# A two-layer graph attention kernel: two small steps of layer 1 move from VectorE to GpSimd

## The chip, the cores and the metric

The kernel runs on one core of a Trainium2 chip. A core has five engines that run their own queues of instructions in order and meet through semaphores: TensorE (matrix products, PE in the profile; its weight loads are PEld), VectorE (DVE), ScalarE (ACT), GpSimd (POOL) and SyncE (SP). Transfers between the chip's memory and the on-chip buffer run on 16 DMA engines. Plain transfers are issued here from SyncE's and ScalarE's queues, gathers by index from GpSimd's. The metric is the device time of one execution in microseconds (us).

## The reference

The reference is one residual block of a graph network: 10,000 nodes with 768 features, 160,000 edges and a self loop per node (each layer adds one more), twice a graph attention layer, and a layer norm over the sum of input and output.

```python
def gat_conv(x, edge_index, W, a_src, a_dst, bias, heads, out_ch, concat):
    ei = _add_self_loops(edge_index, n)
    src, dst = (ei[0], ei[1])
    xl = (x @ W).reshape(n, heads, out_ch)
    alpha_src = jnp.einsum('nhc,hc->nh', xl, a_src)
    alpha_dst = jnp.einsum('nhc,hc->nh', xl, a_dst)
    e = jax.nn.leaky_relu(alpha_src[src] + alpha_dst[dst], 0.2)
    m = jax.ops.segment_max(e, dst, num_segments=n)
    e = jnp.exp(e - m[dst])
    s = jax.ops.segment_sum(e, dst, num_segments=n)
    alpha = e / (s[dst] + 1e-16)
    msg = xl[src] * alpha[:, :, None]
    out = jax.ops.segment_sum(msg, dst, num_segments=n)
...
h = gat_conv(x, edge_index, W1, a_src1, a_dst1, b1, HEADS, HID, True)     # 4 heads of 256
h = jax.nn.relu(layer_norm(h, g1, be1)) + (h0 @ Wr1 + br1)
h1 = h
h = gat_conv(h, edge_index, W2, a_src2, a_dst2, b2, 1, OUT_DIM, False)    # 1 head of 768
h = layer_norm(h, g2, be2) + (h1 @ Wr2 + br2)
...
x = _layernorm(x + h)
```

For every node the sources of its incoming edges are looked up, their projected rows are weighted by a softmax over those edges, and summed.

## The kernel before

The work has three stages, one after the other. All of it is in float32.

**Preparation** (to about 890 us). The nodes are sorted by their number of incoming edges and dealt into 79 tiles of 128 nodes, one node a partition; all nodes of a tile get the same number of places, `SLOTS[t]`, which is that of its largest node. Small tiles have 9 to 14 places, the middle ones 15 to 20, and the largest 21 to 41. `slots` is an integer array with a column for each place of each tile: which row the place is to fetch. Meanwhile `x @ W1` is computed tile by tile and written to `table1`, one row a node. Such a row has R1 = 1033 numbers: 1024 of the projected node, 4 logits as a destination, 4 logits as a source, and in the last column the node's rank in the sorted order, negated.

**Layer 1** (`ordered_layer1`, about 890 to 3,395 us). The tiles are taken in an order that goes from the small ones to the largest and back to small ones (`TURNS`). For a tile, each place's 128 rows are fetched by one gather (`gather`, L425, on GpSimd's queue) into one slot of a ring of 29 slots (`Ring`). The ring runs ahead of the work: when a slot's row has been used, `ring.fetch` issues the gather that refills it with the row 29 places later. A gather therefore waits for the last instruction that reads the slot's old row.

`logits` (L473) forms, over all places of a tile, the sum of source and destination logits (L479), the leaky ReLU (L189), the maximum (L483), the difference (L486) and, on ScalarE, the exponential (L487). It then handles two things for later, in each contiguous part of the ring that the tile's rows take (one part, or two where the ring wraps): the last column of the gathered rows is turned into integers and put into `slots` (L490), so that layer 2 fetches by rank from its own sorted table; and the last five columns of the slots, source logits and rank, are set to a large negative number (L491), so that a later place that fetches no row weighs nothing. `normalised` divides by the sum (L498 to L504).

Of a tile's rows, the first one to four (`on_pe`) are summed on TensorE with diagonal matrices of their weights (diagonals by ScalarE, L730; products, L736). The other rows are added on VectorE by `weigh`: one in four by four multiply-adds straight from the ring (L521), the other three by an addition (L517) after ScalarE has multiplied the row by its weights (L510). After a tile's sum come its layer norm and residual on VectorE (L579 to L595, L807), the transposes of the result (L708, L709), and the products with the layer-2 weights (L829). The residual's product with `Wr1` (L172) runs on TensorE as well.

The order on each engine's queue is that of the program text; no scheduler moves anything. The text sets the weights of the next tile early, while the present one still has three rows to weigh:

```python
if n - LEAD <= k < n - LEAD + 2:
    ready += itertools.islice(ahead, 1)     # first logits of t + 1, then its normalised weights
if k >= first:
    weigh(acc, ring.slot(FIRST[t] + k), e[:, k], DH1, shared=shared(t, k))
ring.fetch(FIRST[t] + k + 1 + ring.size)
```

The one tile with more places than the ring has slots (41) goes through `attend_parts`, which calls `logits` for a part of its places at a time.

**Layer 2** (`ordered_layer2`, to the end). It fetches rows of its own table by the rewritten `slots`, with a ring of 41 slots whose own-node rows come by plain transfers; there `ring.own` holds entries, and the two steps of L490 and L491 are left out. A second path for graphs that don't fit the sorted form (`general_path`) isn't taken with these inputs.

Of the kernel before, what the change touches and what calls it, by code (L numbers as in the profile page):

```python
# [32 lines left out]
OP = mybir.AluOpType  # L33
# [4 lines left out]
BIG = 1.0e30  # L38
# [42 lines left out]
def gnn_kernel(ctx, tc, x, x_cols, src, dst, src_col, dst_col, W1, a_src1, a_dst1, b1, g1, be1, Wr1, br1,  # L81
               W2, a_src2, a_dst2, b2, g2, be2, Wr2, br2, out, n_edges):
    nc = tc.nc
# [6 lines left out]
    R1, R2 = C1 + 2 * H1 + 1, C2 + 2 * H2  # L90
    NT = -(-N // P)
    NP = NT * P
# [40 lines left out]
    slots = consts.tile([P, TOTAL], I32, name="slots")  # L133
# [54 lines left out]
    def leaky(to, a):  # L188
        nc.vector.scalar_tensor_tensor(to, a, SLOPE, a, op0=OP.mult, op1=OP.max)  # L189
# [283 lines left out]
    def logits(small, ring, lo, hi, ad, heads, c, top=None):  # L473


        n = hi - lo
        e = small.tile([P, ring.size, heads], F32, name="e")[:, :n]
        for a, b, rows in ring.parts(lo, hi):
            nc.vector.tensor_tensor(e[:, a - lo:b - lo], rows[:, :, c + heads:c + 2 * heads],  # L479
                                    ad[:, None, :].to_broadcast([P, b - a, heads]), op=OP.add)  # L480
        leaky(e, e)
        new = small.tile([P, heads], F32, name="new")
        nc.vector.reduce_max(new, e.rearrange("p k h -> p h k"), axis=AX.X)  # L483
        if top is not None:
            nc.vector.tensor_max(new, new, top)
        nc.vector.tensor_tensor(e, e, new[:, None, :].to_broadcast([P, n, heads]), op=OP.subtract)  # L486
        nc.scalar.activation(e, e, AF.Exp)  # L487
        for a, b, rows in ring.parts(lo, hi):
            if not ring.own:
                nc.vector.tensor_scalar(slots[:, a:b], rows[:, :, R1 - 1], -1.0, float(NP), op0=OP.mult, op1=OP.min)  # L490
                nc.vector.memset(rows[:, :, c + heads:], -BIG)  # L491
        return e, new

    def normalised(small, e, heads, t):
# [29 lines left out]
    def attend_parts(small, ring, acc, h_, ad, heads, dh, t, summed, between):  # L524
# [6 lines left out]
        nc.vector.memset(acc[:, :c], 0.0)  # L531
        for lo, hi in zip(cuts, cuts[1:]):
            e, new = logits(small, ring, lo, hi, ad, heads, c, top)
            if lo == FIRST[t]:
                doubled(e, t)
# [150 lines left out]
    def ordered_layer1():  # L686
        nc.scalar.add_instruction(mybir.InstLoadActFuncSet(name=nc.get_next_instruction_name(), act_func_set_id=6, engine=nc.scalar.engine))
        with tc.tile_pool(name="b1", bufs=1) as pool, tc.tile_pool(name="small1", bufs=2) as small, \
# [52 lines left out]
            def weights_of(t):  # L741

                n, m = SLOTS[t], on_pe(t)
                e, _ = logits(small, ring, FIRST[t], FIRST[t] + n, ring.slot(FIRST[t])[:, C1:C1 + H1], H1, C1)
                yield e
                normalised(small, e, H1, t)
                acc = ps_acc.tile([P, 2 * BANK], F32, name="acc")
                diagonals = pool.tile([P, ON_PE1 * H1, P], F32, name="diagonals")
                for lo, hi in ((0, min(m, 2)), (min(m, 2), m)):
                    summed(acc, diagonals, e, FIRST[t], lo, hi, m)  # L750
                    yield acc
# [129 lines left out]
    def ordered_layer2():  # L881
# [6 lines left out]
        with tc.tile_pool(name="b2", bufs=1) as pool, tc.tile_pool(name="small2", bufs=2) as small, \  # L888
# [44 lines left out]
            def weights_of(t):  # L933
# [15 lines left out]
                def add_b2():  # L949
                    nc.tensor.matmul(to, ones, b2_b[0:1, ON_PE2:], start=False, stop=False, skip_group_check=True)  # L950

                e, top = logits(small, ring, at, at + cuts[1], ad, H2, C2)
                yield {0: (e, None)}
                if len(cuts) == 2:
# [387 lines left out]
```

## Time and profile before

| | |
|---|---|
| median of 3 runs | 5602.67 us (5597.33 to 5605.57) |
| profiled execution | 5607.1 us, span from first to last instruction 5605.3 us |
| TensorE, weight loads, VectorE | 4888.6 (87%), 2899.2 (52%), 4294.8 us (77%) busy |
| ScalarE, GpSimd | 2813.9 (50%), 3242.1 us (58%) busy |
| granted TensorE clock, mean | 0.93 |
| gathers into the ring (both layers) | 2675, 0.994 us each on GpSimd |
| L490 and L491 on VectorE | 124 each, 24.4 and 13.0 us |
| transfers | 1591 MB, 284 GB/s in the mean |

A group row of the profile gives line, engine, operation, the tiles written and read, their shapes and how often; after the bar the busy time and the mean of one in ns; after the second bar how long the engine had been idle just before such instructions, and what ended that idle time ("issue" is nothing that the profile shows). The shares are means over the three stages. In layer 1 VectorE's share is about 92% in most stretches of 100 us, and TensorE's 93 to 98% in many.

### The profile page before, as it was taken

How to read it: one execution, taken by the hardware profiler on the slowest of the kernel's cores; microseconds unless marked ns; L12 is line 12 of the kernel's file. 1: busy time of each engine (PE TensorE's matmuls, PEld its weight loads, DVE VectorE, ACT ScalarE, POOL GpSimd, SP SyncE). 2: the span in 40 equal slices, each digit the busy share in tenths (PEclk: the TensorE clock that was granted, in tenths of full speed). 3: DMA queues.
4: the chain of work that ended last, by engine and by line, in shares of the span. 5: the costliest groups of instructions: out<-in, count | busy, mean ns of one | idle time of the engine just before them, and what ended most of it. 6: DMA issues, size and time to landing. Idle time of an engine off the chain costs nothing. (4 is left out here: it accounts for less than half of the span.)

```text
span 5605.3 us, 59627 instructions
## 1 busy us (share of the span) xinstructions
PE 4888.6 (87%) x15188; PEld 2899.2 (52%) x15191; DVE 4294.8 (77%) x7761; ACT 2813.9 (50%) x8193; POOL 3242.1 (58%) x3159
## 2 busy tenths in 40 slices
PE   8999996999999875789999999899988888877765
PEld 3444443555555543455555555565655555555544
DVE  5783344999999887888999995888876866766676
ACT  3443344777788776777877773333322322222222
POOL 3447365556666556566666553666665666666664
PEclk9999998999999987899999999999998888888877
DMA  4333626999999987899999986999888888888885
GB/s 156 122 99 87 92 90 254 323 335 352 362 361 373 340 320 265 316 343 360 364 359 355 335 307 231 323 336 331 320 321 292 313 299 299 288 293 286 289 286 182
DMA packets 474307, 1591.37 MB, mean 284 GB/s; under 512 B 118328, under 2 KB 122488, under 8 KB 473959
## 3 DMA queue, kind: packets, MB, share of 16 engines
q0 software_dynamic: 322384, 1286.62, 64.8%
q1 hardware_dynamic: 149520, 297.43, 15.8%
q10 hardware_dynamic: 2054, 3.42, 0.2%
q8 instruction: 128, 2.10, 0.2%
q14 instruction: 221, 1.80, 0.1%
HBM read 1431.80 MB, written 177.29 MB: 287 GB/s over the span
## 5 line engine op out<-in xcount | busy, mean ns | idle before, releaser
L425 POOL DMA_INDIRECT ring<-table,slots x2675 | 2660.2, 994 | 1774.4 <-issue 542.1
L521 DVE SCALAR_TENSOR_TENSOR acc<-ring,e,acc 128x512 f32<-128x512 f32 (+1 forms) x2530 | 1578.3, 624 | 137.7 <-PE acc L736 46.1
L510 ACT ACTIVATE ring<-ring,e 128x256 f32<-128x256 f32 x3284 | 1338.3, 508 | 1.4 <-issue 1.2
L517 DVE TENSOR_TENSOR acc<-acc,ring 128x1024 f32<-128x1024 f32 x801 | 985.7, 1231 | 73.2 <-issue 1.9
L991 PE MATMUL big<-wr,w 128*128 128x512 f32 (+1 forms) x2464 | 876.7, 502 | 147.0 <-issue 145.5
L946 PE MATMUL big<-ring,diagonals 128*128 128x256 f32 x2754 | 746.9, 430 | 169.1 <-issue 138.7
L172 PE MATMUL big<-w,xT 128*128 128x512 f32 x1896 | 823.8, 596 | 26.5 <-DMA w<-in_W_dram 10.3
L172 PE MATMUL big<-wr,xT 128*128 128x512 f32 x1896 | 833.2, 596 | 0.2 <-issue 0.2
L829 PE MATMUL half<-w,hT 128*128 128x512 f32 (+1 forms) x2528 | 830.4, 486 | 0.0
L946 PEld LDWEIGHTS big<-ring,diagonals 128*128 128x128 f32 x2754 | 590.5, 218 | 331.3 <-issue 203.6
L991 PEld LDWEIGHTS big<-wr,w 128*128 128x128 f32 x2464 | 484.2, 197 | 504.0 <-issue 471.6
L945 ACT ACTIVATE diagonals<-ident,e 128x128 f32<-128x128 f32 x1377 | 423.9, 388 | 612.9 <-remote 230.0
L829 PEld LDWEIGHTS half<-w,hT 128*128 128x128 f32 x2528 | 477.8, 189 | 372.3 <-issue 332.7
L736 PE MATMUL acc<-ring,diagonals 128*128 128x256 f32 x1912 | 480.1, 408 | 204.8 <-ACT diagonals L730 179.6
L172 PEld LDWEIGHTS big<-w,xT 128*128 128x128 f32 x1896 | 361.3, 191 | 484.5 <-issue 466.3
L172 PEld LDWEIGHTS big<-wr,xT 128*128 128x128 f32 x1896 | 356.7, 192 | 420.3 <-issue 420.3
L736 PEld LDWEIGHTS acc<-ring,diagonals 128*128 128x128 f32 x1912 | 387.0, 205 | 290.7 <-ACT diagonals L730 200.8
L583 ACT ACTIVATE sd<-mv,eps 128x1 f32<-128x1 f32 x237 | 69.3, 292 | 697.5 <-DVE mv L581 451.6
L730 ACT ACTIVATE diagonals<-ident,e 128x128 f32<-128x128 f32 x956 | 293.0, 387 | 207.6 <-DVE e L501 165.4
L667 DVE TENSOR_TENSOR scr<-big,ad_b 128x1024 f32<-128x1024 f32 x79 | 96.7, 1224 | 377.5 <-ACT row L664 333.4
L672 POOL TENSOR_TENSOR row<-row,none 128x1024 f32<-128x1024 f32 x79 | 187.2, 2370 | 260.8 <-ACT row L664 258.4
L670 ACT ACTIVATE scr<-scr 128x256 f32<-128x256 f32 x632 | 253.6, 402 | 120.3 <-DVE scr L667 117.7
(185 smaller groups left out, 3430.6 us busy)
## 6 DMA issues: line engine op xcount, KB each, us to landing
ring<-table,slots POOLq DMA_INDIRECT x2675
table<-row SPq DMA_DIRECT2D x79, 516.0 KB
h_d<-hT SPq DMA_DIRECT2D x79, 512.0 KB
w<-h_d SPq DMA_DIRECT2D x77, 512.0 KB
table<-row SPq DMA_DIRECT2D x79, 385.0 KB
ring<-table SPq DMA_DIRECT2D x79, 385.0 KB
xT<-in_x_cols_dram SPq DMA_DIRECT2D x79, 384.0 KB
x_d<-xt SPq DMA_DIRECT2D x79, 384.0 KB
```

Source lines behind the costliest of these rows:

```text
L172: nc.tensor.matmul(p[:, c:e], aT[:, j, :], w[:, j, c:e], start=(j == 0), stop=(j == k - 1))
L425: nc.gpsimd.indirect_dma_start(out=to, out_offset=None, in_=table, in_offset=bass.IndirectOffsetOnAxis(ap=index, axis=0), **more)
L510: nc.scalar.activation(row[:, s], row[:, s], AF.Copy, scale=e[:, h:h + 1])
L517: nc.vector.tensor_add(acc[:, :c], acc[:, :c], row[:, :c])
L521: nc.vector.scalar_tensor_tensor(acc[:, s], row[:, s], e[:, h:h + 1], (acc if first is None else first)[:, s], op0=OP.mult, op1=OP.add)
L670: nc.scalar.activation(m[:, s], m[:, s], AF.Copy, accum_out=row[:, C1 + i * H1 + h:C1 + i * H1 + h + 1])
L730: nc.scalar.activation(diagonals[:, k * H1 + i, :], ident, AF.Copy, scale=e[:, k, i:i + 1])
L736: nc.tensor.matmul(acc[:, c:d], diagonals[:, k * H1 + i, :], ring.slot(q + k)[:, c:d], start=(k == 0 and c % BANK == 0), stop=(k == m - 1 ...
L829: nc.tensor.matmul(q, hT[:, j, :], w2[:, j, c:c + q.shape[1]], start=(j == 0), stop=(j == K1 - 1))
L945: nc.scalar.activation(diagonals[:, (k - lo) % G, :], ident, AF.Copy, scale=e[:, k - lo, :])
L946: nc.tensor.matmul(to, diagonals[:, (k - lo) % G, :], ring.slot(at + k)[:, ON_PE2:C2], start=False, stop=(k == n - 1), skip_group_check=True)
L991: nc.tensor.matmul(r[:, c:d], hT[:, j, :], wr2[:, j, c:d], start=False, stop=(j == K1 - 1 and d < C2), skip_group_check=True)
```

## The change

In `logits`, the two instructions that prepare layer 2 and clear the used logit columns are issued on GpSimd's queue in place of VectorE's. Their operands, their number (124 each) and their place in the program text stay. On GpSimd's queue they stand between ring gathers.

```diff
         for a, b, rows in ring.parts(lo, hi):
             if not ring.own:
-                nc.vector.tensor_scalar(slots[:, a:b], rows[:, :, R1 - 1], -1.0, float(NP), op0=OP.mult, op1=OP.min)
-                nc.vector.memset(rows[:, :, c + heads:], -BIG)
+                nc.gpsimd.tensor_scalar(slots[:, a:b], rows[:, :, R1 - 1], -1.0, float(NP), op0=OP.mult, op1=OP.min)
+                nc.gpsimd.memset(rows[:, :, c + heads:], -BIG)
         return e, new
```

The waits that follow from it: on GpSimd the first of the two waits for the gathered rows, the second for the first and for VectorE's reading of the logits (L479). The gather that refills a slot, which waited for VectorE's fill of it, now waits for GpSimd's own.

## The prediction

> **What bounds the kernel now.** I read the windows first, to see which engine is full while layer 1 runs (about 890 to 3,395 us); then the groups by line, for the two instructions that move; then the waits of GpSimd and of TensorE; last the timeline of one tile.
>
> Three stretches of 100 us, one with small tiles, one with the largest and one with middling tiles (columns: length, busy us of TensorE, its weight loads, VectorE, ScalarE and GpSimd, the granted clock, the DMA share, GB/s):
>
> ```profile
> 1080.00:1180.00 100.00, 98.17 (x333) 58.08 (x332) 92.56 (x155) 74.74 (x199) 57.92 (x57) 1.00 0.93 332
> 2080.00:2180.00 100.00, 73.08 (x250) 47.00 (x248) 84.98 (x150) 76.56 (x207) 64.30 (x59) 0.86 0.72 256
> 2680.00:2780.00 100.00, 96.01 (x324) 57.06 (x323) 90.90 (x149) 79.22 (x214) 64.98 (x63) 1.00 1.00 368
> ```
>
> VectorE shows 85 to 93 us of 100 and the timeline has it back to back (the rest is some 0.03 to 0.1 us between two instructions), so 93 is full. TensorE at 96 to 98 is as full. The kernel is balanced between the two, and GpSimd, at 58 to 65, is full nowhere. The instructions that move, the wait for ring rows, and rows that price an instruction on GpSimd:
>
> ```profile
> L490 DVE TENSOR_SCALAR slots<-ring 128x8 int32<-128x8 f32 (+20 forms) x124 | 24.4, 197 | 0.9
> L491 DVE MEMSET ring<- 128x40 f32 (+20 forms) x124 | 13.0, 105 | 7.5
> ...
> L479 DVE TENSOR_TENSOR e<-ring 128x32 f32<-128x32 f32 (+22 forms) x119 | 21.5, 200 | 70.4 <-DMA ring<-table,slots 65.0 <-issue 5.1
> ...
> L672 POOL TENSOR_TENSOR row<-row,none 128x1024 f32<-128x1024 f32 x79 | 187.2, 2370 | 260.8 <-ACT row L664 258.4 <-issue 1.8
> ...
> masks.py:197 POOL MEMSET ident<- 128x128 f32 x1 | 0.2, 205 | 0.3 <-POOLq L1334 0.3
> ```
>
> The 124 pairs cost VectorE 24.4 + 13.0 us of work. Who waits in layer 1, GpSimd first (us in total, times, longest), then TensorE:
>
> ```profile
> POOL ring L425 <- DVE e L504: 156.6, 69, 7.0
> ...
> PE acc L736 <- ACT diagonals L730: 179.6, 49, 24.9
> PE half L708 <- ACT xT L709: 27.3, 46, 1.0
> PE half L708 <- DVE h L807: 24.3, 13, 2.3
> ```
>
> And one tile of 15 rows about the place that changes (VectorE and GpSimd from the timeline: start, length, engine):
>
> ```profile
> 1216.92 0.99 POOL L425 DMA_INDIRECT ring<-table,slots  x1 [0.34 <-issue]
> ...
> 1217.49 0.39 DVE L490 TENSOR_SCALAR slots<-ring 128x15 int32<-128x15 f32 x1
> ...
> 1217.96 0.12 DVE L491 MEMSET ring<- 128x75 f32 x1
> 1218.00 1.21 DVE L517 TENSOR_TENSOR acc<-acc,ring 128x1024 f32<-128x1024 f32 x1
> ...
> 1219.48 0.99 POOL L425 DMA_INDIRECT ring<-table,slots  x1 [1.57 <-DVE e L504]
> ```
>
> Two things are to be seen. First, VectorE's L490 takes 0.39 us and ends at 1217.88, just as GpSimd's gather ends at 1217.91. In 62 of the 111 L490 entries of the timeline a gather runs alongside, and they average 0.26 us, many ending within 0.03 us of it; the 49 without average 0.14. VectorE is held there until GpSimd is done. Second, GpSimd then sits idle for 1.57 us until VectorE has weighed one more row (L517), because the next gather overwrites that row's slot. The wait is put down to L504, which is what VectorE runs next.
>
> **What the change removes.** From the start of the first L490 of a tile to VectorE's next instruction I read 81 places in the timeline: 36.9 us in sum, 0.46 on average (0.26 for the smallest tiles, 0.67 with two parts while a gather runs). That is what leaves VectorE's queue. L486, ScalarE's exponential and L504 keep their order; the exponential, 0.25 us, still has a weighed row (1.21 us) in front of L504, so no new wait appears there.
>
> **Where this shortens the path.** A tile's period runs from one L807 to the next. Only where TensorE has room does a faster VectorE shorten it. In every tile TensorE waits about 0.47 us for ScalarE's copy of a transpose (L708 behind L709), which VectorE doesn't set; what it idles beyond this I count as room, and a tile gains the smaller of its removed time and its room. By rows in a tile (tiles: period, removed in sum, mean room, gain in sum):
> up to 14 (19 tiles): 25.1, 6.7, 0.65, gain 3.2;
> 15 (8): 28.3, 4.7, 1.65, gain 3.8;
> 16 (7): 28.4, 3.6, 0.19, gain 1.3;
> 17 (8): 29.6, 4.0, 1.23, gain 4.0;
> 18 (7): 30.4, 3.4, 0.29, gain 1.5;
> 19 and 20 (13): 32.6, 5.9, 1.96, gain 5.9;
> 21 and more (16): 43.6, 8.1, 10.3, gain 8.1.
> The sum is 27.7 us. At 14, 16 and 18 rows TensorE has just been given one more row (L736), is full, and the gain is lost as a VectorE wait for its result. The large tiles wait for rows as well (36 of the 65 us that L479 waits for ring rows); since VectorE frees the slots that the gathers refill, its earlier finish moves that loop too, and I take the whole 8.1 (bound: nothing). Their 256 to 335 GB/s, against 368 elsewhere, say that it is delay and not the transfer rate that they wait for.
>
> **What GpSimd takes on.** The order of the changed kernel has both instructions between the gather that waits for the last weighed row before the logits and the gather that waits for the first one after them. L490 waits for rows, in 33 of 124 cases by a semaphore of its own; VectorE's L479 waits for the same rows, and no gather behind L490 can run before VectorE is past L479, so nothing queued behind it (the tile's next ring gathers; the gather of x comes later) loses by that. L491 waits for L479 and for L490. No trace row has this form on GpSimd. Below: 0.10 us, its smallest fill. Above: 2.37 us, its 128x1024 addition with two inputs. I take 0.2 us each, its fill of 128x128, as 1 to 130 elements a partition are nearest to that. A tile with one part then has about 0.5 us in an idle stretch of 1.57 less the 0.46 by which VectorE's row comes sooner, so it is hidden. With two parts it is about 1.0 us in the same 1.1: the end of the second L491 can meet VectorE's L504. For that I charge 0.1 us at 30 places, 3 us. Without the cover, the delay meets the next idle stretch (1.72 us) before it reaches any row. The changed order also gives L479 a wait for GpSimd's fills; that is for a fill a whole round of the ring back, done long before. 31 more wait steps on VectorE at the 17 ns that such a step takes on GpSimd's queue are 0.5 us.
>
> Sum: 27.7 - 3 - 0.5 = 24 us less. The profiled execution took 5607.1 us (span 5605.3), 4.4 over the median 5602.67; taken from the median: 5579 us.
>
> The Trainium skill, "GPSIMD Engine Reference", section "Engine selection", speaks against the change: elementwise work belongs on VectorE, GpSimd being about half as fast with two inputs and near line rate with one. The trace agrees for two (2.37 us against VectorE's 1.22 for 1024 elements). By that rule L490 and L491 would cost 0.2 to 0.35 us, an estimate, which changes the sum by nothing as long as they sit in idle time. "SBUF — State Buffer", section "Who interferes with whom", says that a VectorE instruction with one tensor in the fast two-port mode locks out GpSimd and is locked out by it; that fits L490's 0.39 us, and would make the removal worth more than its 0.17 us of work.
>
> **The rivals.** A: the gain is absorbed. TensorE is as full as VectorE, and where the DMA share is 1.00 (19 and 20 rows, 368 GB/s) earlier gathers may land no earlier. Without the 8.1 and the 5.9 the sum is 27.7 - 14 - 3.5 = 10 us: 5592, no change that shows. For it: the 17 tiles without any room. Against: L479 waits for rows only 2 us in those 13 tiles.
> B, slower: GpSimd gets late. In a tile of n rows it issues n + 1 gathers at 1.29 us (0.99 and a gap of 0.30). At 18 rows that is 24.5 of 30.4 us, so it bounds the tile once the pairs take over 5.9 us, 3.7 a pair with 1.57 pairs a tile. At the upper price of 4.7 a pair (7.4 a tile) tiles of 16 to 20 rows lose 1 to 1.7 us, 46 us in all, of which the gain in the rest gives back about 10: 5639. Against: 0.2 us rows for much larger tiles.
> C, slower: GpSimd's new work holds VectorE as its gathers do now. Two holds of 0.25 us (0.39 less 0.14) per pair are 62 us, less 36.9: 5628. It decides from 0.15 us a hold. Against: L517, which runs beside it, keeps its 1.21 to 1.23 us beside every gather.
>
> **How the numbers follow.** This kernel's measurement can tell about 0.2%, 11 us, from no change. Chances: forecast 0.60, with its own range 5565 to 5590; A 0.24; B 0.08; C 0.08. The low end is the whole 36.9 us off and the spread of the runs below the median (5 us): 5561. The high end, 5610, takes in A with no gain left and a loss of 7 us from holds; beyond it lie B and C, some 0.16, and 0.02 lies below. Faster 0.62 (the forecast and a little of A), same 0.22, slower 0.16.
>
> **What the next profile should show.** L490 and L491 as GpSimd rows of about 0.1 to 0.3 us, VectorE's busy time some 37 us lower, the GpSimd wait behind L504 shorter than 156.6 us by about a half, tiles of 15, 17, 19 and 20 rows about 0.45 us shorter, tiles of 14, 16 and 18 unchanged. Wrong if these GpSimd rows exceed 1 us, if L479, L189 or L486 grow beside them, or if L479's wait for rows grows by what VectorE saved.

## The result, and the profile after

The changed kernel takes 5572.26 us (median of 7 runs, 5563.30 to 5584.64) against 5602.67 us before (7 runs, 5597.33 to 5607.92). The two medians lie 30 us apart; the ratio on record, by which this document goes, is 0.9953, 95% interval 0.9942 to 0.9964: 26 us less, between 20 and 33. The forecast was 5579 us, 24 less, in a range of 5561 to 5610. The profiled execution took 5572.26 us, with a span of 5570.4 us.

The windows of the same three stretches after the change (same columns as before: length, busy us of TensorE, weight loads, VectorE, ScalarE, GpSimd, granted clock, DMA share, GB/s):

```profile
1080.00:1180.00 100.00, 98.17 (x334) 57.99 (x333) 91.46 (x142) 75.24 (x200) 59.10 (x70) 1.00 0.93 339
2080.00:2180.00 100.00, 62.04 (x207) 40.23 (x205) 81.08 (x136) 67.95 (x185) 67.38 (x65) 0.80 0.67 243
2680.00:2780.00 100.00, 96.64 (x350) 60.83 (x349) 90.97 (x137) 81.21 (x224) 69.23 (x74) 1.00 1.00 370
```

In the first and third, TensorE and VectorE are about as full as they were and GpSimd has 1 to 4 us more of 100. The second is another moment of the large tiles, as the kernel runs ahead, so its shares are not to be set beside those of before. Balance did not change; the gain must be sought in the places. The groups of the moved instructions and of their neighbours:

```profile
L490 POOL TENSOR_SCALAR slots<-ring 128x8 int32<-128x8 f32 (+20 forms) x124 | 38.4, 310 | 25.0 <-DMA ring<-table,slots 15.6 <-issue 1.0
L504 DVE TENSOR_SCALAR e<-e,loops 128x4 f32<-128x4 f32 (+1 forms) x158 | 34.1, 216 | 3.0 <-remote 1.6 <-issue 0.7 <-ACT e L487 0.7
L491 POOL MEMSET ring<- 128x40 f32 (+20 forms) x124 | 18.9, 152 | 30.0 <-DVE e L479 22.4
...
L479 DVE TENSOR_TENSOR e<-ring 128x32 f32<-128x32 f32 (+22 forms) x119 | 21.7, 200 | 74.6 <-DMA ring<-table,slots 66.0 <-issue 3.8 <-POOL ring L491 2.6
```

L490 and L491 are now GpSimd rows of 310 and 152 ns in the mean (medians 280 and 147). L504, which the prediction feared would be held, went from 213 to 216 ns. L479's waiting for gathered rows stands at 66.0 us against 65.0. The waits in layer 1 (us in total, times, longest):

```profile
PE acc L736 <- ACT diagonals L730: 198.0, 45, 29.4
DVE acc L521 <- PE acc L736: 46.5, 44, 4.3
POOL ring L425 <- DVE e L504: 35.5, 24, 3.0
POOL ring L491 <- DVE e L479: 22.4, 3, 8.8
PE half L708 <- DVE h L807: 18.8, 12, 2.7
```

GpSimd's wait behind L504 went from 156.6 to 35.5 us. A part of that is a change of name, as what is left of such a wait now often stands under "issue" (as in the tile below); of GpSimd's waits ahead of ring gathers that are put to "issue" there were 262.1 us before and are 334.4 now. VectorE's wait for TensorE's sums (L521 behind L736) is 46.5 us. Before, it was this:

```profile
DVE acc L521 <- PE acc L736: 46.1, 41, 4.8
```

So what VectorE saved did not come back as such a wait. The place itself, in a tile of 15 rows (timeline: start, length, engine):

```profile
1218.62 0.99 POOL L425 DMA_INDIRECT ring<-table,slots  x1 [0.35 <-issue]
...
1219.06 0.22 DVE L486 TENSOR_TENSOR e<-e,new 128x60 f32<-128x60 f32 x1
1219.20 1.23 DVE L517 TENSOR_TENSOR acc<-acc,ring 128x1024 f32<-128x1024 f32 x1
...
1219.68 0.30 POOL L490 TENSOR_SCALAR slots<-ring 128x15 int32<-128x15 f32 x1
...
1220.04 0.17 POOL L491 MEMSET ring<- 128x75 f32 x1
...
1220.33 0.22 DVE L504 TENSOR_SCALAR e<-e,loops 128x4 f32<-128x4 f32 x1
...
1220.82 1.06 POOL L425 DMA_INDIRECT ring<-table,slots  x1 [0.61 <-issue]
```

VectorE goes from L486 straight into the next weighed row; GpSimd does its two instructions in what was idle time and still has 0.61 us to spare ahead of the next gather.

**Where the time went, by stage.** From the first to the last L807, layer 1 took 2471.5 us in the profiled execution of before and 2465.0 in a second one (b1_before_again, below); of the changed kernel there are three, 2446.6, 2446.8 (e4_again) and 2445.0 us (e10_changed). The means differ by 22 us; the two executions of before lie 6.5 us apart, so this is good to some 3 us. Layer 2, from the first to the last L1005, took 2098.9 and 2063.8 us before, and 2085.6, 2105.4 and 2087.0 after: it moves by 35 us between the two executions of before, so single traces can't say whether it adds anything. Layer 1 is much steadier, and I compare kernels there. By rows in a tile, as differences of these means, with the prediction's gains beside them:

| rows (tiles) | predicted | measured |
|---|---|---|
| up to 14 (19) | -3.2 | -3.3 |
| 15 (8) | -3.8 | -3.7 |
| 16 (7) | -1.3 | -3.2 |
| 17 (8) | -4.0 | -3.5 |
| 18 (7) | -1.5 | -2.7 |
| 19 and 20 (13) | -5.9 | -6.3 |
| 21 to 27 (15), 41 (1) | -8.1 together | -4.2 and +4.8 |
| charges for GpSimd and wait steps | +3.5 | none seen |
| sum | -24.2 | -22.1 |

(The time between two L807 counts for the tile whose rows are weighed in it.) Not all rows of the table are equally firm. Against the mean of before, the three executions of the changed kernel give -3.1 to -3.3 us at 16 rows, but -1.9 to -3.6 at 18 and -3.3 to -4.8 in the 15 tiles of 21 to 27 rows, where the two executions of before differ by 3.1 themselves.

### The profile page after: what moved, and what is told of

The parts are those of the page before. It is cut to its first block, busy times and chain, and to the rows that moved or that the text cites. A ratio compares the mean times of both kernels' runs of the same rounds, so it can differ in the third digit from the quotient of the medians.

```text
span 5570.4 us, 59760 instructions
## 1 busy us (share of the span) xinstructions
PE 4887.3 (88%) x15188; PEld 2896.9 (52%) x15191; DVE 4269.6 (77%) x7513; ACT 2815.1 (51%) x8193; POOL 3301.6 (59%) x3407
## 5 line engine op out<-in xcount | busy, mean ns | idle before, releaser
L521 DVE SCALAR_TENSOR_TENSOR acc<-ring,e,acc 128x512 f32<-128x512 f32 (+1 forms) x2530 | 1579.0, 624 | 149.4 <-PE acc L736 46.5
L517 DVE TENSOR_TENSOR acc<-acc,ring 128x1024 f32<-128x1024 f32 x801 | 986.5, 1232 | 70.5 <-DVE acc L517 1.4
L946 PE MATMUL big<-ring,diagonals 128*128 128x256 f32 x2754 | 758.5, 433 | 206.8 <-issue 168.0
L829 PEld LDWEIGHTS half<-w,hT 128*128 128x128 f32 x2528 | 477.8, 189 | 372.3 <-issue 334.4
L736 PE MATMUL acc<-ring,diagonals 128*128 128x256 f32 x1912 | 474.8, 406 | 201.9 <-ACT diagonals L730 198.0
L736 PEld LDWEIGHTS acc<-ring,diagonals 128*128 128x128 f32 x1912 | 384.6, 204 | 285.0 <-ACT diagonals L730 219.0
```

Of the source, the lines that this page charges most:

```text
L517: nc.vector.tensor_add(acc[:, :c], acc[:, :c], row[:, :c])
L521: nc.vector.scalar_tensor_tensor(acc[:, s], row[:, s], e[:, h:h + 1], (acc if first is None else first)[:, s], op0=OP.mult, op1=OP.add)
L736: nc.tensor.matmul(acc[:, c:d], diagonals[:, k * H1 + i, :], ring.slot(q + k)[:, c:d], start=(k == 0 and c % BANK == 0), stop=(k == m - 1 ...
L829: nc.tensor.matmul(q, hT[:, j, :], w2[:, j, c:c + q.shape[1]], start=(j == 0), stop=(j == K1 - 1))
L946: nc.tensor.matmul(to, diagonals[:, (k - lo) % G, :], ring.slot(at + k)[:, ON_PE2:C2], start=False, stop=(k == n - 1), skip_group_check=True)
```

## The experiments

Changes below are "layer 1" differences against the first profiled execution of before, unless said otherwise; the second one of before stands at -6.5 us on that scale, the changed kernel at -24.6 to -26.5. Times and ratios are against the kernel before, run on the same chip at the same time. Some kernels came to a chip on which the kernel before takes 5265.5 us. In the traces from there layer 2 lasts some 1,760 us, and layer 1 has about 8 us more in the tiles of up to 14 rows, so I compare kernels of that chip with each other.

### One half at a time

Only the ranks (L490) on GpSimd, the fill on VectorE:

```diff
                 nc.gpsimd.tensor_scalar(slots[:, a:b], rows[:, :, R1 - 1], -1.0, float(NP), op0=OP.mult, op1=OP.min)
-                nc.gpsimd.memset(rows[:, :, c + heads:], -BIG)
+                nc.vector.memset(rows[:, :, c + heads:], -BIG)
```

> L490 (ranks to slots) on GpSimd, L491 (the fill) stays on VectorE. Theory P, the prediction's: what is saved is VectorE's time at the place where the pair stood, some 0.3 of the 0.46 us by L490, because the fill alone still takes about 0.1 us: 18 to 20 us below the kernel before. Theory H, the hold: nearly all of the saving is that VectorE no longer stands still behind the gather, so this alone gives the whole 26 us, and L491 alone nothing.

Measured: 5651.73 us against 5612.09, ratio 1.0077 (1.0056 to 1.0098); layer 1 +41.3 us. Both expectations missed, in sign too. VectorE's waits in layer 1 of this kernel (us, times, longest):

```profile
DVE ring L491 <- issue: 57.7, 63, 16.2
...
DVE ring L491 <- POOL slots L490: 31.2, 18, 9.1
```

And the timeline of one of its 15-row tiles:

```profile
1232.92 0.99 POOL L425 DMA_INDIRECT ring<-table,slots  x1 [0.35 <-DVE acc L517]
...
1233.36 0.22 DVE L486 TENSOR_TENSOR e<-e,new 128x60 f32<-128x60 f32 x1
...
1233.98 0.30 POOL L490 TENSOR_SCALAR slots<-ring 128x15 int32<-128x15 f32 x1
...
1234.36 0.12 DVE L491 MEMSET ring<- 128x75 f32 x1 [0.78 <-issue]
1234.40 1.21 DVE L517 TENSOR_TENSOR acc<-acc,ring 128x1024 f32<-128x1024 f32 x1
```

The fill overwrites the column that L490 reads, so it must follow it. L490 stands on GpSimd behind a gather that ends at 1233.91; VectorE is ready for the fill at about 1233.58 and starts it at 1234.36, after 0.78 us idle, with the weighed rows behind it in its queue. Over the layer that is 57.7 + 31.2 = 89 us of waiting. Moving half of the pair is worse than moving none.

Only the fill (L491) on GpSimd, the ranks on VectorE:

```diff
-                nc.gpsimd.tensor_scalar(slots[:, a:b], rows[:, :, R1 - 1], -1.0, float(NP), op0=OP.mult, op1=OP.min)
+                nc.vector.tensor_scalar(slots[:, a:b], rows[:, :, R1 - 1], -1.0, float(NP), op0=OP.mult, op1=OP.min)
                 nc.gpsimd.memset(rows[:, :, c + heads:], -BIG)
```

> L491 on GpSimd, L490 stays on VectorE. Theory P: 124 fills of about 0.1 us leave VectorE, three quarters of them where it counts: 7 to 10 us below the kernel before. Theory H: no more than 3 us, and L490 still lasts 0.26 us on average when a gather runs beside it.

Measured: 5592.39 us against 5612.09, ratio 0.9968 (0.9956 to 0.9981); layer 1 -16.1 us. That is about twice the 7 to 10 of the prediction's theory, and far more than the 3 of theory H. The timeline of this kernel shows why (a tile in two parts):

```profile
1249.10 0.38 DVE L490 TENSOR_SCALAR slots<-ring 128x8 int32<-128x8 f32 x2
...
1249.25 1.36 DVE L517 TENSOR_TENSOR acc<-acc,ring 128x1024 f32<-128x1024 f32 x1
1249.53 0.19 POOL L491 MEMSET ring<- 128x40 f32 x2
```

L490 is still held while a gather runs beside it (0.23 us an instruction, against 0.17 without), but the weighed row L517 reads nothing that L490 writes and starts 0.15 us after L490's beginning. Before, VectorE's own fill stood between them, and it waits for L490's end. The time from the end of L486 to VectorE's next other instruction sums, over the layer, to 30.3 us before, 4.3 here and -4.2 in the changed kernel (negative: the next one starts before L486 has quite ended). So most of the place was the fill and its wait for L490's end.

To see whether it is the wait that makes half a move a loss, the ranks were left on GpSimd and VectorE's fill was put one weighed row later, at the head of `normalised`:

```diff
-                nc.gpsimd.memset(rows[:, :, c + heads:], -BIG)
+                fills.append(rows[:, :, c + heads:])
...
     def normalised(small, e, heads, t):
+        fill()                              # nc.vector.memset of what stands in fills
```

(The 41-row tile has its fills at once, as in e1.)

> As e1, L490 on GpSimd and the fill on VectorE, but the fill is issued one weighed row later, at the head of the normalisation. If e1 lost its 41 us in layer 1 because the fill has to wait for GpSimd's L490, which stands behind a gather, this wait is now over by the time VectorE gets there: what remains is L490's share, 15 to 20 us off layer 1 and off the time (0.3% below the kernel before). If L490 on GpSimd is costly by itself, the time stays above the kernel before.

Measured: 5582.77 us against 5591.17, ratio 0.9985 (0.9970 to 1.0000); layer 1 -12.1 us, which is -23.4 without the 41-row tile (+11.3), where the fill still follows at once. The fill's group row in this kernel (its line is L477 here, L490's is L496):

```profile
L477 DVE MEMSET ring<- 128x40 f32 (+20 forms) x124 | 11.0, 105 | 33.8 <-issue 18.0 <-POOL slots L496 15.1
```

Its waiting fell from 89 us to 33.8. The same instruction on the same engine, one row later: the loss of e1 was the wait. The 15 to 20 us that were expected are reached outside the 41-row tile only. The whole time is 0.15% lower where 0.3% was expected, with an interval that reaches no change.

### Neither, and how much there was to gain

Both instructions left out; layer 2 then fetches by the node's own number and used columns keep their logits:

```diff
             if not ring.own:
-                nc.gpsimd.tensor_scalar(slots[:, a:b], rows[:, :, R1 - 1], -1.0, float(NP), op0=OP.mult, op1=OP.min)
-                nc.gpsimd.memset(rows[:, :, c + heads:], -BIG)
+                pass
```

> Both instructions are left out (layer 2 then fetches as many rows, but by node number, and the used columns are not cleared), so that neither VectorE nor GpSimd has the work: the ceiling of the change. Theory P with the prediction's room on TensorE: 28 us below the kernel before, 2 to 4 below the changed kernel. Theory R, that TensorE is not the limit in tiles of 14, 16 and 18 rows: all 36.9 us of VectorE's time, 35 to 37 below the kernel before. If GpSimd's share of the work cost something in the changed kernel, this one is over 5 us below it.

Measured: 5582.13 us against 5612.09, ratio 0.9943 (0.9925 to 0.9961); layer 1 -31.1 us. The 30 us are near theory P's 28 and short of theory R's 35 to 37. The changed kernel once more, beside it on the same chip:

> The changed kernel once more, for a second trace and a second comparison. If the 10 us by which its trace was shorter in layer 2 (turns 70 to 75) belong to the change, they are there again, and the time is 30 us below the kernel before; if they are the spread between executions, layer 2 takes 2193 us as before, give or take 10, and the time is 22 to 27 below. The tile of 41 rows again takes 4 to 5 us longer than the 81.0 us before, if that is GpSimd's instructions standing behind VectorE's there.

Measured: 5590.32 us, ratio 0.9956 (0.9940 to 0.9973); layer 1 -24.6 us. The two differ by 6.5 us in layer 1, of which 5.6 lie in the one 41-row tile (-0.7 without the pair, +4.9 with it). Over all other tiles together the pair on GpSimd costs as good as nothing (-30.4 against -29.6), and that tile is where the rest is. This holds for the sum: in single traces groups of tiles differ either way (tiles of 21 to 27 rows -8.5 without the pair and -4.9 with it, tiles of 18 rows -0.4 and -2.9).

### How much room GpSimd has

Idle fills on GpSimd after each pair, into a buffer that nothing reads: six of 256 numbers a partition (2.15 us a pair with the gaps between them; with the pair itself 2.6 us, at 1.57 pairs a tile 4.1 us a tile), and fourteen (5.1 us, so 5.6 a pair and 8.8 a tile).

```diff
                 nc.gpsimd.memset(rows[:, :, c + heads:], -BIG)
+                for _ in range(6):          # 14 in e8_filler_long
+                    nc.gpsimd.memset(idle, 0.0)
```

> The changed kernel with six more fills of 256 numbers on GpSimd behind each pair, some 0.3 us each by its fill of 128 numbers (0.2 us): about 1.8 us, so 2.4 us a pair. Theory B of the prediction, that a whole tile's idle time on GpSimd can be used: 18 rows need 24.5 + 1.57 x 2.4 = 28.3 of 29.8 us, no loss but in the tile of 41 rows (about 6 us). Theory L, that only the idle stretch in front of the next gather (0.65 us are left there) can be used: 1.2 us too much with one part, 3 with two, some 130 us in all.

> The same with fourteen fills, about 4.2 us, so 4.8 us a pair and 7.5 a tile. Theory B: tiles of 16 to 20 rows are bound by GpSimd, which needs 29.4, 30.7, 32.0, 33.3 and 34.6 us there against 27.9, 29.1, 30.0, 31.2 and 32.5: some 65 us above the changed kernel. Theory L: some 3.5 to 8 us in each tile, over 300 us above it.

Both ran on the other chip, beside e7_large_on_vector (below), which takes 5233.38 us there. Measured: six fills 5268.71 us, ratio to before 1.0013 (1.0003 to 1.0023); fourteen 5458.43 us, 1.0367 (1.0348 to 1.0386). The fills' group in the kernel with six (busy us, mean ns, idle before):

```profile
L494 POOL MEMSET idle<- 128x256 f32 x744 | 232.0, 312 | 35.5
```

and in the kernel with fourteen:

```profile
L494 POOL MEMSET idle<- 128x256 f32 x1736 | 540.5, 311 | 92.4
```

The wait for gathered rows of the kernel with fourteen (lines are one higher here, as a buffer was added; L480 is L479):

```profile
DVE e L480 <- DMA ring<-table,slots: 213.7, 43, 27.2
```

and the same wait in e7_large_on_vector:

```profile
DVE e L479 <- DMA ring<-table,slots: 80.1, 23, 26.8
```

Against e7_large_on_vector, in us per tile:

| rows | 15 | 16 | 17 | 18 | 19 and 20 |
|---|---|---|---|---|---|
| 4.1 us of added work a tile | 0.1 | 0.2 | 0.1 | 0.2 | 0.8 |
| 8.8 us of added work a tile | 2.1 | 3.6 | 2.7 | 4.9 | 3.8 |
| by rival B's sum, with 8.8 us | 1.6 | 2.9 | 2.8 | 3.5 | 3.0 |

The prediction's rival B put the point from which GpSimd bounds an 18-row tile at 5.9 us of added work. At 4.1 us the tiles of 15 to 18 rows lose next to nothing; at 8.8 all of these lose, from 0.1 us less than the sum says (17 rows) to 1.4 us more (18 rows), and VectorE's wait for gathered rows is 213.7 us, against 80.1 in e7_large_on_vector. The change itself adds 0.46 us a pair, some 0.7 us a tile, an eighth of that threshold. So in these tiles the slack is nearer to that of the whole tile than to that of the one idle stretch about L504: 2.6 us a pair is far beyond that stretch, which the timelines of the changed kernel give as 1.2 us with one part and 1.75 with two.

Neither theory gives the totals. Six fills cost 35 us against e7_large_on_vector, which is more than the whole gain of the change, where theory B had some 6 and theory L 130. In layer 1 that is 32 us: 9.9 in the 41-row tile (some 5 of them the pair itself, as below), 9.7 in tiles of 19 and 20 rows (0.8 us each, where the sum has 1.6 to spare), 6.1 in tiles of 21 to 27 rows and 6.6 in the rest. Fourteen fills cost 225 us against the same kernel, 223 of them in layer 1, where theory B had 65 (154 by its sum with the measured 8.8 us) and theory L over 300; 38 us of it lie in tiles of 21 to 27 rows, where the sum has 9. What the fills cost beyond the sum is not explained. Room on GpSimd in the mean of a tile is thus not free of cost everywhere.

### VectorE's hold beside a gather

The pair on VectorE as before, but L490 in a form with a second tensor (of constants) in place of a number:

```diff
-                nc.gpsimd.tensor_scalar(slots[:, a:b], rows[:, :, R1 - 1], -1.0, float(NP), op0=OP.mult, op1=OP.min)
-                nc.gpsimd.memset(rows[:, :, c + heads:], -BIG)
+                nc.vector.scalar_tensor_tensor(slots[:, a:b], rows[:, :, R1 - 1], -1.0, limit[:, :b - a], op0=OP.mult, op1=OP.min)
+                nc.vector.memset(rows[:, :, c + heads:], -BIG)
```

> The kernel before, with L490 written on VectorE as an operation on two tensors (the limit as a tensor of constants), which does the same. If what holds VectorE is that L490's form and the running gather exclude each other, L490 no longer ends with the gather: 0.17 us with or without one beside it, and layer 1 is 5 to 8 us shorter. If any access to the ring waits there, L490 still averages 0.26 us beside a gather. Its fill of constants and the time of the run say nothing more.

Measured: 5259.72 us in a single run against 5265.5, which the times can't tell from no change. The group row of this kernel:

```profile
L492 DVE SCALAR_TENSOR_TENSOR slots<-ring,limit 128x8 int32<-128x8 f32 (+20 forms) x124 | 19.0, 153 | 0.9
```

The mean is 153 ns against 197, and the longest of the 124 is 188 ns against 410 before: the hold is gone, though a gather still runs beside 78 of them (0.16 us in the mean, 0.14 beside none). The time from the end of L486 to VectorE's next other instruction sums to 25.0 us here, against 30.3 before, so some 5 us of it were the hold. Tiles of 15 rows and more are shorter by 6.5 us together against the first execution of before, 3.8 against the mean of its two; the changed kernel gains 21.4 and 18.7 there (mean of three). So the hold is real, and by itself about a fifth to a third of the gain. This share is no firmer than that: the run was on the other chip, and one and the same kernel (e7 below) takes 4 us more there in these tiles than on the first kind.

### The 41-row tile

The changed kernel, except that the one tile that goes through `attend_parts` keeps its pairs on VectorE:

```diff
-    def logits(small, ring, lo, hi, ad, heads, c, top=None):
+    def logits(small, ring, lo, hi, ad, heads, c, top=None, mover=nc.gpsimd):
...
-            e, new = logits(small, ring, lo, hi, ad, heads, c, top)
+            e, new = logits(small, ring, lo, hi, ad, heads, c, top, nc.vector)
```

> The changed kernel, but the tile of 41 rows, which takes its rows in three goes, keeps both instructions on VectorE. In that tile GpSimd issues gathers back to back and its two instructions stood up to 2 us behind VectorE's. If that is what it cost, the tile takes 80 to 81 us again in place of 85.5, layer 1 2442 us in place of 2446.7, and the time is 29 to 30 us below the kernel before. If the rows of that tile are late for another reason, the tile still takes 85.

Measured: 5233.38 us against 5265.5, ratio 0.9940 (0.9926 to 0.9954); that tile -0.3 us. As the changed kernel had not run on that chip, both were run on one of the first kind, and the kernel before once more:

> The changed kernel with the tile of 41 rows left to VectorE, beside the changed kernel on the same chip: its tile of 41 rows 5 us shorter, layer 1 29 to 31 us shorter than in the kernel before, the rest alike. The 5 us are 0.1% of the time, below what the times alone can tell.

> The changed kernel beside the next one on the same chip. Layer 1, from the first L807 to the last, takes 24 to 26 us less than in the kernel before; the time is 0.44 to 0.47% below it.

> The kernel before once more, for a second trace: layer 1 takes 2471.5 us give or take 2, the same in each tile; layer 2 differs by up to 10 us from the first trace, which is what a difference there has to exceed to mean anything.

Measured: e7_again 5565.53 us, 0.9956 (0.9940 to 0.9972), layer 1 -32.9, the tile -0.6; the changed kernel 5566.68 us, 0.9951 (0.9933 to 0.9970), layer 1 -26.5, the tile +4.5; the kernel before 5569.62 us in that single run (its median was 5591.17), layer 1 -6.5 and layer 2 -35, both beyond the 2 and 10 us that were expected. In the traces the variant is 6 us shorter, 5 of them in that tile; the whole times do not separate it from the changed kernel, so it can't be called faster. That the pairs on GpSimd cost this tile some 5 us is shown by two runs of the variant without them, and by e3 (-0.7). What happens there, in the changed kernel's timeline:

```profile
2135.69 4.83 DVE L521 SCALAR_TENSOR_TENSOR h<-ring,e,h 128x256 f32<-128x256 f32 x12
...
2137.38 1.24 POOL L425 DMA_INDIRECT ring<-table,slots  x1 [0.30 <-PE acc L736]
2138.69 1.99 POOL L490 TENSOR_SCALAR slots<-ring 128x14 int32<-128x14 f32 x1
...
2140.74 0.17 POOL L491 MEMSET ring<- 128x70 f32 x1
2141.55 1.23 POOL L425 DMA_INDIRECT ring<-table,slots  x1 [0.65 <-POOL ring L491]
```

This tile sums in `h`, which lies in the on-chip buffer and not, like `acc`, in the accumulators that TensorE writes. L490 takes 1.99 us while VectorE's multiply-adds on `h` (L521) run, and ends 0.16 us after them; the gathers behind it are late. In the layer's timeline, L490 averages 0.28 us beside additions into `acc` (93 of them, at most 0.34) and 1.38 us beside those into `h` (three: 0.82, 1.32 and 1.99). L491's wait for L479 in this tile's first part (7.5 us, at 2106.9) is not what costs: the next gather after it waits 2.75 us more for VectorE's L521. That the stretched L490 and the gathers behind it make up the 5 us is argued from these rows; no run took away the stretch alone.

## Why the prediction was right, point by point

The total was right: 24 us forecast, 26 measured (20 to 33), of which 22 can be placed in layer 1. Some of its terms were not.

- *VectorE's place, 36.9 us.* Right. The two groups, 37.4 us, are gone, and the gap after L486 shrank by 34.5 us (30.3 to -4.2). The sign that was listed for it, VectorE's busy time some 37 us lower, came at 25.2 us (4294.8 to 4269.6): instructions overlap at their ends (in the tile that the prediction shows, L490 starts at 1217.49 and L486, before it, ends at 1217.57), which is at least a part of the difference.
- *The hold of L490 behind a gather.* Right as a fact (e6), but it is not the larger part of the place (some 5 of 30.3 us): e2 leaves the hold and keeps most of the gain. I had not seen that the fill, in waiting for L490, is what passes the hold on to the weighed row.
- *GpSimd at 0.2 us each.* Taken together 0.40, measured 0.46; L490 under-priced (0.31), L491 over-priced (0.15). The estimate of 0.2 to 0.35 us was wrongly worked out: it doubles VectorE's 0.10 and 0.17 us, but the Trainium skill's "GPSIMD Engine Reference", section "Engine selection", has the factor of two for two inputs and "roughly line-rate" for one. L490 has one tensor as its input and took a median of 0.28 us, against VectorE's 0.14 without a gather beside it; L491 has none and took 0.147, against 0.105.
- *One part 0.5 us, two parts 1.0 us of the idle stretch.* Right: 0.54 and 1.04 us from L490's start to L491's end, with 0.62 and 0.66 us left (medians). The charge of 3 us for two parts that meet L504 was wrong: with two parts the idle stretch measures 1.75 us, not the 1.1 that I had for both, and L504 grew by 0.4 us in sum.
- *No new wait that matters.* Right for the ordinary tiles. The wait of L479 for a fill "done long before" came once, 2.6 us. L491 waited for L479 three times, 22.4 us in sum: once in the 41-row tile, ahead of a gather that wasn't due for 2.75 us more, and twice in the last tiles, where no ring gather follows.
- *A tile gains the smaller of its removed time and TensorE's room.* Right for the tiles of up to 14 rows together and at 15, 17, 19 and 20 (0.44 to 0.48 us a tile, near the 0.45 listed for the next profile), wrong at 16 rows: 3.2 us, where 1.3 were forecast and "unchanged" was listed. The tiles gained 0.45 us each, nearly what was removed. At 18 rows it is 2.7 us against 1.5, 0.39 a tile, but there the executions scatter from 1.9 to 3.6 and e3, which has no such work at all, stands at 0.1. The tiles of 14 rows, listed as unchanged too, were 0.22 us shorter each. "The gain is lost as a VectorE wait" is the step that failed: that wait stood at 46.1 us and is 46.5. In the traces TensorE's idle time between two L807 fell at 16 rows from 0.90 to 0.64 us a tile, which is 0.26 of the 0.45, and its busy time in the same window fell by 0.2 us (27.4 to 27.2), with fewer transposes (L708) in the window: 13.3 a tile in place of 14.9 and 14.0. So the window that the prediction counted in is not TensorE's own tile, and its work in it is no fixed amount. That TensorE lags in one tile and catches up in a neighbour would fit this, but it is argued, and no run shows it.
- *The largest tiles give all of 8.1 us.* Wrong, and it was the largest miss: 4.2 us in 15 of them and a loss of 4.8 in the 41-row tile. The one tile seems to be most of it: with its pairs on VectorE (e7_again, one trace) the sixteen tiles give 7.6 us, nearly the 8.1. The row for it was in the profile of before: in that tile VectorE's instructions take both inputs from the on-chip buffer, and gathers beside them took up to 2.44 us. There rival C, a hold between GpSimd's new work and VectorE, came true with the sides reversed: GpSimd is held.
- *The wait behind L504 down by half.* Further: from 156.6 to 35.5 us, less than a quarter, a part of it by a change of name to "issue".

So the terms at 16 and 18 rows (3.1 us too little) and the charges (3.5 us too much) nearly made up for the large tiles (8.7 us too much). The mechanism was right and the closeness is partly luck. Of the rivals, A (absorbed, 10 us, a ratio of 0.9982) lies above the intervals of all three comparisons of the changed kernel (upper ends 0.9964, 0.9973 and 0.9970); B did not occur, but e5 and e8 put its threshold, for tiles of 15 to 18 rows, between 4.1 and 8.8 us a tile, with the 5.9 that was worked out in between; C is confined to one tile.

## What to carry to other kernels

Of two instructions of which the second overwrites what the first reads, don't move the first alone: moving both off a full engine gained 26 us, moving only the second some 20, and moving only the first lost 40, since the engine that was to be relieved then waited for a queue full of gathers. Price the work on the new engine against its slack over a whole period (gathers times their spacing against the tile), and not only against the idle stretch beside it. A slack in the mean is no promise: six idle fills a pair stayed within it at 15 to 18 rows and still cost 35 us in all. And look for the one tile that is built differently: here 1 of 79 tiles gave back 5 us, most likely because its sum lies in another memory.

## What the runs showed of the hardware

- VectorE's L490 with one tensor and two numbers is stretched beside a GpSimd gather (up to 410 ns); with two tensors it isn't (at most 188 ns). This fits what the Trainium skill's "SBUF — State Buffer", section "Who interferes with whom", says of the fast two-port modes, which it lists `tensor_scalar` among; no run shows the mode in which L490 ran.
- The other way round, GpSimd is slowed by VectorE instructions with two inputs in the on-chip buffer. The same section says that these contend with GpSimd instructions that read that buffer, which fits L490's 1.99 us. It adds, as inferred, that they do not stall the gathers' descriptor work; here gathers, which read their indices from that buffer, took 1.28 us in the mean beside additions into `h` (27 of them, up to 2.47), against 1.00 beside those into `acc` (1,159, at most 1.11), and likewise in the kernel before (1.25, up to 2.44, against 0.99).
- Layer 2 of one and the same kernel lasted 2063.8 us in one execution and 2098.9 in another, and about 1,760 on another chip, where layer 1 stayed within some 15 us (2450.8 against 2438.6 us for e7). A change of 20 us in one stage is best read from that stage.
